# Routed experts in steps of two pairs of pages, in a hybrid block with two mixture-of-experts layers

## The chip, the cores and the metric

The kernel runs on one core of a Trainium2 chip. The metric is the device time of one execution in microseconds (us); three executions of the kernel before took 1439.03, 1439.33 and 1444.63 us, so its median is 1439.33 us. Five engines share the work: PE (TensorE, matrix products and transposes, with its weight loads shown as PEld), DVE (VectorE), ACT (ScalarE), POOL (GpSimd) and SP (SyncE, which here issues most DMA transfers). Each engine takes its instructions in order, and waits where an operand, a buffer or a bank of PSUM is not ready.

## The reference

`x` has shape 4 x 1024 x 256 in float32, so there are 4096 tokens of width 256. The block is

```python
x = x + attn_a(layernorm(x))     # RWKV time mixing
x = x + ffn(layernorm(x))        # mixture of experts, layer 1
x = x + attn_b(layernorm(x))     # retention, 16 heads
x = x + ffn(layernorm(x))        # the same experts, layer 2
```

and the part that is changed is the routed half of `ffn`, with E = 64 experts of inner width F = 64, of which each token takes K = 4:

```python
scores = softmax(flat @ router_w)
_, topk_idx = top_k(flat @ router_w + router_bias, 4)
comb = the four scores of each token, scaled to sum 1, at the chosen experts
g = silu(einsum('nd,edf->nef', flat, wg)); u = einsum('nd,edf->nef', flat, wu)
routed = einsum('ne,nef,efd->nd', comb, g * u, wd)
shared = two shared experts of width 256, for every token
```

## The kernel before

**Pages and pairs.** The 4096 tokens are handled in 8 segments of 512. A token's normalized row is sent, by four indirect writes from POOL (L429), to rows of a buffer in memory called `sent`, in pages of 128 rows where each page belongs to one expert. Two pages make a pair. Pair p is loaded, computed and stored as a unit by `routed` (L518), and the results land in a second buffer, `made`. Afterwards `gather` (L593) fetches four rows for each token back with indirect reads from POOL (L606), and DVE adds them into `x` with their weights (L617). How many pairs hold what segments 0 to i have sent is `until(i)`; the kernel uses the list `USUAL` (L75), 33, 38, 43, 51, 59, 67, 75, 83, when the drawn routing fits in it, which it does here in both layers (83 pairs each: 1328 instructions of L554 are 2 layers x 83 pairs x 8). A second arm of the program, not taken here, uses the worst case of 96 pairs.

**One pair.** `load` (L522) reads the two expert numbers of the pair, then has SP issue three DMA transfers: the rows `rx` (256 KB, L530) and the packed weights of its two experts `rw` (two of 192 KB, L532). `up` (L537) turns the rows with four PE transposes into one bank of PSUM (`rt`), which DVE copies to `rxT` (L546). `mid` (L549) multiplies by the gate and up weights (`rg`, half a bank: 2 pages x 128 columns), ACT takes silu of the gate half (`rs`, L559), DVE multiplies it by the up half (`rh`, L562), and ACT copies the product to the upper 64 partitions (L563), so that two products can use the two halves of the PE rows. `down` (L566) multiplies by the down weights into two half-filled banks (`rp`), which are copied to `ry` (L581): the first by ACT, the second by DVE for the first `until(0)` pairs and by ACT later. ACT then issues the store of 256 KB to `made` (L582).

**What sets the order.** `step(p)` (L584) records load(p), up(p-2), mid(p-3), down(p-4) at position p of a track, and `merge` (L54) interleaves tracks by their positions: in layer 1 with the gathers and with the retention batches, which start at position `until(0) + 14`; in layer 2 with the gathers, the stores of the output and the shared experts (`shared`, L446: L457, L462, L463, L470). From that recorded order a scheduler builds each engine's final order by its own model of durations, so neighbours can change places. A new tile of a tag waits until the tile that had its buffer is no longer read. `deep` gives the counts of buffers: in layer 1, (4, 2, 4) for `rx` and `rw`, for `ry`, and for the gathered rows; in layer 2, (6, 4, 6). `rxT`, `rs` and `rh` have two buffers each. Tag B has three banks of PSUM, used by `rt`, by both `rp` halves and by other stages; tag A has four.

`beat` (L79) notes a DVE instruction, and `on_beat` (L83) makes a POOL gather wait for the last one noted.

Of the kernel before, what the change touches and what calls it, by code (L numbers as in the profile page):

```python
# [10 lines left out]
F32 = mybir.dt.float32  # L11
# [10 lines left out]
P = 128  # L22
D = 256
KC = D // P
# [24 lines left out]
def track(steps, lo, hi):  # L49

    return [(lo + (hi - lo) * n / len(steps), step) for n, step in enumerate(steps)]
# [9 lines left out]
def hybrid_kernel(ctx: ExitStack, tc: tile.TileContext, a: dict, out: bass.AP):  # L61
# [94 lines left out]

    def pairs_until(i):

        return min(NPAIR, (((i + 1) * SEG * TOPK + E * (P - 1)) // P + 1) // 2)

    PACE, LAG = 2, 7.0

# [80 lines left out]
    class Ffn:  # L243
# [273 lines left out]

        def routed(self, pool, until):  # L518

            st, first, last = {}, until(0), until(NSEG - 1)  # L520

            def load(p):  # L522
# [7 lines left out]
                nc.sync.dma_start(out=x, in_=sent[p * P : (p + 1) * P])  # L530
                for j, e in enumerate(got):
                    nc.sync.dma_start(  # L532
# [1 line left out]
                    )  # L534
                st[p] = dict(x=x, w=w)

            def up(p):  # L537
                nm, s = f"{self.name}{p}", st[p]
                tp = bank("B", f"rt_{nm}", [P, KC, 2, P])
                for j in range(2):  # L540
                    for k in range(KC):
                        nc.tensor.transpose(  # L542
                            tp[:, k, j, :], s["x"][:, j, k * P : (k + 1) * P], ident
                        )
                xT = pool.tile([P, KC, 2, P], F32, tag="rxT", bufs=2, name=f"rxT_{nm}")
                beat(nc.vector.tensor_copy(out=xT, in_=tp))  # L546
                s["xT"] = xT

            def mid(p):  # L549
                nm, s = f"{self.name}{p}", st[p]  # L550
                gu = bank("A", f"rg_{nm}", [P, 2, P])
                for j in range(2):
                    for k in range(KC):
                        nc.tensor.matmul(  # L554
                            gu[:, j, :], lhsT=s["w"][:, j, k * 2 * F : (k + 1) * 2 * F],
                            rhs=s["xT"][:, k, j, :], start=(k == 0), stop=(k == KC - 1),
                        )
                act = pool.tile([P, 2, P], F32, tag="rs", bufs=2, name=f"rs_{nm}")
                nc.scalar.activation(out=act[F:], in_=gu[:F], func=AF.Silu)  # L559

                h = pool.tile([P, 2, P], F32, tag="rh", bufs=2, name=f"rh_{nm}")
                beat(nc.vector.tensor_mul(out=h[:F], in0=gu[F:], in1=act[F:]))  # L562
                nc.scalar.copy(out=h[F:], in_=h[:F])  # L563
                s["h"] = h

            def down(p):  # L566
                nm, s = f"{self.name}{p}", st.pop(p)
                y = pool.tile([P, 2, D], F32, tag="ry", bufs=self.deep[1], name=f"ry_{nm}")
                halves = [bank("B", f"rp_{nm}_{c}", [P, 2, P]) for c in range(2)]
                for j in range(2):  # L570

                    for c, yp in enumerate(halves):
                        r = slice(c * F, (c + 1) * F)
                        nc.tensor.matmul(  # L574
                            yp[:, j, :], lhsT=s["h"][r, j, :], rhs=s["w"][r, j, WD:],
                            start=True, stop=True,
                        )
                for c, yp in enumerate(halves):

                    copy = nc.vector.tensor_copy if c and p < first else nc.scalar.copy  # L580
                    copy(out=y[:, :, c * P : (c + 1) * P], in_=yp)  # L581
# [9 lines left out]
            return track([lambda p=p: step(p) for p in range(last + 4)], 0, last + 4)  # L591

        def gather(self, i, pool, until):  # L593


            nm, s = f"{self.name}{i}", self.pick[i]
            ready = [min(until(NSEG - 1), until(i) + PACE * t) for t in range(TT)]
            got = {}

            def fetch(t, k):  # L600
# [716 lines left out]
```

## Time and profile before

The profiled execution took 1439.49 us. Its span, from the first instruction to the last, is 1437.3 us; the rest, 2.2 us, lies around it.

| what | value |
|---|---|
| median of three executions | 1439.33 us (1439.03 to 1444.63) |
| profiled execution, and its span | 1439.49 us, 1437.3 us |
| stage with the time mixing and the first routing | about 0 to 385 us |
| layer 1, routed pairs nearly alone | about 390 to 520 us |
| layer 1, routed pairs among the retention batches | about 520 to 790 us |
| rest of the retention, routing for layer 2 | about 790 to 1120 us |
| layer 2, routed pairs and shared experts | about 1120 to 1411 us |
| last gathers, additions and stores | about 1411 to 1437 us |

The borders come from where the groups of L542, L554 and L574 are busy, asked in stretches of 20 us. A row of the groups' view has the line, the engine, the operation, the tile written and the tiles read, its size and count, then busy time, mean duration in ns, and the engine's idle time just before such instructions with what ended it. A matrix product in float32 runs as two PE instructions, so one `rg` product counts twice. PE durations in the groups overlap each other, since PE is pipelined; the chain of waits, which follows the last instruction back to what released each step, shows how long a run of them really holds the engine.

### The profile page before, as it was taken

The numbers are of one execution on the slowest core, as the hardware profiler recorded it, in microseconds if no ns is written. First come the engines' busy times: TensorE is split into PE (matmuls) and PEld (weight loads), VectorE is DVE, ScalarE is ACT, GpSimd is POOL, SyncE is SP. The second block draws the span as 40 slices with busy tenths as digits, with TensorE's granted clock in tenths as the row PEclk, the third lists the DMA queues.
The fourth block names the chain that finished last, engine by engine and source line by source line (L and its number), as shares of the span: only waits on it lengthen the run. The fifth ranks groups of instructions, "written<-read, shape, count | busy, mean of one in ns | idle before, by whom it ended". The sixth has DMA issues, their size and how long they took to land. (4 is left out here: it accounts for less than half of the span.)

```text
span 1437.3 us, 23813 instructions
## 1 busy us (share of the span) xinstructions
PE 1263.5 (88%) x7872; PEld 894.5 (62%) x7872; DVE 993.9 (69%) x2495; ACT 741.6 (52%) x1424; POOL 526.1 (37%) x536
## 2 busy tenths in 40 slices
PE   6899999999298879999999889699998799999993
PEld 2455555555277657777776666467465577777772
DVE  6999989998255447766666777886774355476664
ACT  7989898964044445556644463353431234444440
POOL 0043245545400144424224304536707000277565
PEclk9899999999699999999999999699999799999997
DMA  9976931112599976567453201212202798999984
GB/s 350 403 247 81 294 105 59 59 44 78 177 311 326 341 278 196 185 202 248 140 169 114 61 31 49 74 45 93 88 12 103 246 319 283 310 377 386 362 316 130
DMA packets 192297, 276.26 MB, mean 192 GB/s; under 512 B 53795, under 2 KB 119718, under 8 KB 192166
## 3 DMA queue, kind: packets, MB, share of 16 engines
q1 hardware_dynamic: 143686, 163.98, 36.0%
q0 software_dynamic: 24576, 67.14, 14.1%
q10 hardware_dynamic: 23904, 43.53, 8.0%
q8 instruction: 65, 1.06, 0.3%
q14 instruction: 66, 0.54, 0.1%
HBM read 166.05 MB, written 121.11 MB: 200 GB/s over the span
## 5 line engine op out<-in xcount | busy, mean ns | idle before, releaser
L606 POOL DMA_INDIRECT gy_f<-made,to_f x256 | 249.7, 975 | 486.8 <-DMA made<-ry_f 145.4
L429 POOL DMA_INDIRECT sent<-xn_f,to_f x256 | 273.4, 1068 | 413.9 <-issue 179.8
L554 PE MATMUL rg_f<-rxT_f,rw_f 128*128 128x128 f32 x1328 | 187.9, 285 | 11.6 <-DVE rxT_f L546 6.6
L554 PEld LDWEIGHTS rg_f<-rxT_f,rw_f 128*128 128x128 f32 x1328 | 167.1, 196 | 22.9 <-DVE rxT_f L546 14.8
L559 ACT ACTIVATE rs_f<-rg_f 64x256 f32<-64x256 f32 x166 | 62.2, 375 | 218.2 <-PE rg_f L554 193.7
L542 PE MATMUL rt_f<-ident,rx_f 128*128 128x128 f32 x664 | 108.0, 286 | 46.8 <-DMA rx_f<-sent 43.3
L574 PE MATMUL rp_f<-rw_f,rh_f 64*128 64x128 f32 x1328 | 140.1, 301 | 9.4 <-DVE S L1021 3.6
L546 DVE COPY rxT_f<-rt_f 128x512 f32<-128x512 f32 x166 | 114.3, 688 | 45.7 <-PE rt_f L542 44.2
L581 ACT COPY ry_f<-rp_f 128x256 f32<-128x256 f32 x266 | 92.9, 374 | 99.7 <-DMA made<-ry_f 50.5
L617 DVE SCALAR_TENSOR_TENSOR x<-gy_f,w_f,x 128x256 f32<-128x256 f32 x256 | 122.3, 482 | 14.3 <-DMA gy_f<-made,to_f 9.8
L457 PE MATMUL g_f<-xnT_f,f_swg 128*128 128x512 f32 x256 | 129.4, 623 | 0.6 <-ACT sh_f L462 0.6
L470 PE MATMUL o_f<-f_swd,sh_f 128*128 128x256 f32 x512 | 121.5, 385 | 8.2 <-DVE sh_f L463 4.3
L574 PEld LDWEIGHTS rp_f<-rw_f,rh_f 64*128 64x128 f32 x1328 | 103.4, 188 | 38.3 <-ACT ry_f L581 7.9
L457 PE MATMUL u_f<-xnT_f,f_swu 128*128 128x512 f32 x256 | 122.3, 595 | 0.7 <-DVE sh_f L463 0.7
L542 PEld LDWEIGHTS rt_f<-ident,rx_f 128*128 128x128 f32 x664 | 76.4, 144 | 71.5 <-issue 36.0
L562 DVE TENSOR_TENSOR rh_f<-rg_f,rs_f 64x256 f32<-64x256 f32 x166 | 70.7, 426 | 62.7 <-ACT rs_f L559 59.7
L470 PEld LDWEIGHTS o_f<-f_swd,sh_f 128*128 128x128 f32 x512 | 95.0, 191 | 29.9 <-DVE sh_f L463 6.7
L683 PE MATMUL rvk<-xnT_a,rvk 128*128 128x512 f32 x192 | 92.5, 629 | 7.1 <-DVE xnT_a L240 6.6
L1056 DVE TENSOR_TENSOR pm<-sc,decay 128x512 f32<-128x512 f32 x128 | 82.9, 681 | 17.9 <-PE sc L1035 17.7
L463 DVE TENSOR_TENSOR sh_f<-u_f,sh_f 128x512 f32<-128x512 f32 x64 | 43.8, 686 | 62.5 <-PE u_f L457 56.4
L462 ACT ACTIVATE sh_f<-g_f 128x512 f32<-128x512 f32 x64 | 38.0, 596 | 92.4 <-PE g_f L457 50.5
L563 ACT COPY rh_f<-rh_f 64x256 f32<-64x256 f32 x166 | 66.8, 403 | 33.9 <-DVE rh_f L562 29.7
(238 smaller groups left out, 2160.9 us busy)
## 6 DMA issues: line engine op xcount, KB each, us to landing
rw_f<-wx SPq DMA_DIRECT2D x332, 192.0 KB
rx_f<-sent SPq DMA_DIRECT2D x166, 256.0 KB
made<-ry_f ACTq DMA_DIRECT2D x166, 256.0 KB
sent<-zeros SPq DMA_DIRECT2D x7, 2048.0 KB
sent<-zeros SPq DMA_DIRECT2D x1, 10240.0 KB
x<-in_x_dram SPq DMA_DIRECT2D x8, 512.0 KB
wx<-in_wg_dram SPq DMA_DIRECT2D x2, 2048.0 KB
sent<-xn_f,to_f POOLq DMA_INDIRECT x256
```

Source lines behind the costliest of these rows:

```text
L429: ins = nc.gpsimd.indirect_dma_start(out=rows_sent[: pairs_until(i) * 2 * P, :], out_offset=bass.IndirectOffsetOnAxis(ap=st["to"][:, c : c ...
L457: nc.tensor.matmul(ps, lhsT=w[:, k, s], rhs=self.xnT[i][:, k, :], start=(k == 0), stop=(k == KC - 1),)
L470: nc.tensor.matmul(o[:, t, :], lhsT=st["h"][:, c, s], rhs=self.weights[2][:, c, :], start=(c == 0), stop=(c == NS - 1),)
L542: nc.tensor.transpose(tp[:, k, j, :], s["x"][:, j, k * P : (k + 1) * P], ident)
L546: beat(nc.vector.tensor_copy(out=xT, in_=tp))
L554: nc.tensor.matmul(gu[:, j, :], lhsT=s["w"][:, j, k * 2 * F : (k + 1) * 2 * F], rhs=s["xT"][:, k, j, :], start=(k == 0), stop=(k == KC - 1),)
L574: nc.tensor.matmul(yp[:, j, :], lhsT=s["h"][r, j, :], rhs=s["w"][r, j, WD:], start=True, stop=True,)
L581: copy(out=y[:, :, c * P : (c + 1) * P], in_=yp)
L606: ins = nc.gpsimd.indirect_dma_start(out=got[t][:, k, :], out_offset=None, in_=rows_made[: ready[t] * 2 * P, :], in_offset=bass.IndirectOf ...
L617: tc.keep_in_program_order(nc.vector.scalar_tensor_tensor(out=xs[i][:, t, :], in0=got[t][:, k, :], scalar=s["w"][:, c : c + 1], in1=xs[i][ ...
L683: nc.tensor.matmul(ps, lhsT=rvk[:, k, lo : lo + P], rhs=st["xnT"][:, k, :], start=(k == 0), stop=(k == KC - 1),)
L1056: ins = nc.vector.tensor_mul(out=pm, in0=ch[j]["sc"][g], in1=decay.rearrange("p (k g b) n -> p g k b n", k=KC, b=2)[:, g],)
```

## The change

Two pairs, q and q + 1, now go through `up`, `mid` and `down` together. Loads stay one pair at a time. The counts of pairs are rounded up to even numbers: `USUAL` becomes 34, 38, 44, 52, 60, 68, 76, 84; the worst case stays at 96. `rg`, and each half of `rp`, now fill a bank of 512 columns, and silu, the product, the copy of the product and the copies of `rp` are one instruction for two pairs. The `rt` banks and `rxT` stay one per pair. The store to `made` is one of 512 KB for two pairs. `rs` and `rh` have one buffer of twice the size. `ry` keeps two buffers in layer 1, each twice as large, and has two instead of four in layer 2. The buffers of `rx` and `rw` stay at four pairs in layer 1 and six in layer 2. `step` records, at odd positions p, up(p-3), then down(p-5), then mid(p-3), after load(p). The down products keep the order they are recorded in, after the first.

```diff
-    NPAIR = (NPAGE + 1) // 2
+    NPAIR = 2 * ((NPAGE + 3) // 4)
-    USUAL = [(max(E + 2 + 10 * i, (i + 1) * SEG * TOPK // P + E // 2 + 6) + 1) // 2 for i in range(NSEG)]
+    USUAL = [
+        2 * ((max(E + 2 + 10 * i, (i + 1) * SEG * TOPK // P + E // 2 + 6) + 3) // 4)
+        for i in range(NSEG)
+    ]
...
-                w = pool.tile([P, 2, WD + P], F32, tag="rw", bufs=self.deep[0], name=f"rw_{nm}")
+                w = pool.tile([P, 2, WD + P], F32, tag="rw", bufs=self.deep[3], name=f"rw_{nm}")
...
+            def up(q):
+                for p in (q, q + 1):
...
+            def mid(q):
+                nm = f"{self.name}{q}"
+                gu = bank("A", f"rg_{nm}", [P, 2, 2, P])
+                for i in range(2):
+                    s = st[q + i]
+                    for j in range(2):
+                        for k in range(KC):
+                            nc.tensor.matmul(
+                                gu[:, i, j, :], lhsT=s["w"][:, j, k * 2 * F : (k + 1) * 2 * F],
+                                rhs=s["xT"][:, k, j, :], start=(k == 0), stop=(k == KC - 1),
+                            )
+                act = pool.tile([P, 2, 2, P], F32, tag="rs", bufs=1, name=f"rs_{nm}")
                 nc.scalar.activation(out=act[F:], in_=gu[:F], func=AF.Silu)
-                h = pool.tile([P, 2, P], F32, tag="rh", bufs=2, name=f"rh_{nm}")
+                h = pool.tile([P, 2, 2, P], F32, tag="rh", bufs=1, name=f"rh_{nm}")
                 beat(nc.vector.tensor_mul(out=h[:F], in0=gu[F:], in1=act[F:]))
                 nc.scalar.copy(out=h[F:], in_=h[:F])
...
+                y = pool.tile([P, 2, 2, D], F32, tag="ry", bufs=self.deep[1], name=f"ry_{nm}")
+                halves = [bank("B", f"rp_{nm}_{c}", [P, 2, 2, P]) for c in range(2)]
+                for i in range(2):
+                    for j in range(2):
+                        for c, yp in enumerate(halves):
+                            r = slice(c * F, (c + 1) * F)
+                            ins = nc.tensor.matmul(
+                                yp[:, i, j, :], lhsT=h[r, i, j, :], rhs=two[i]["w"][r, j, WD:],
+                                start=True, stop=True,
+                            )
+                            if i or j or c:
+                                tc.keep_in_program_order(ins)
                 for c, yp in enumerate(halves):
-                    copy = nc.vector.tensor_copy if c and p < first else nc.scalar.copy
-                    copy(out=y[:, :, c * P : (c + 1) * P], in_=yp)
-                nc.scalar.dma_start(out=made[p * P : (p + 1) * P], in_=y)
+                    copy = nc.vector.tensor_copy if c and q < first else nc.scalar.copy
+                    copy(out=y[:, :, :, c * P : (c + 1) * P], in_=yp)
+                nc.scalar.dma_start(
+                    out=made[q * P : (q + 2) * P].rearrange("(i p) j d -> p i j d", p=P), in_=y
+                )
             def step(p):
                 if p < last:
                     load(p)
-                for d, f in ((2, up), (3, mid), (4, down)):
-                    if 0 <= p - d < last:
+                for d, f in ((3, up), (5, down), (3, mid)):
+                    if (p - d) % 2 == 0 and 0 <= p - d < last:
                         f(p - d)
...
-    f1 = Ffn("f1_", pf, keep, (4, 2, 4))
+    f1 = Ffn("f1_", pf, keep, (4, 2, 4, 4))
...
-        f2 = Ffn("f2_", pf, arm.enter_context(tc.tile_pool(name="keep2", bufs=NSEG)), (6, 4, 6))
+        f2 = Ffn("f2_", pf, arm.enter_context(tc.tile_pool(name="keep2", bufs=NSEG)), (6, 2, 6, 6))
```

More of the change, by code (lines that the diff above doesn't have):

```diff
@@ L157, in pairs_until @@
     def pairs_until(i):
-        return min(NPAIR, (((i + 1) * SEG * TOPK + E * (P - 1)) // P + 1) // 2)
+        return min(NPAIR, 2 * ((((i + 1) * SEG * TOPK + E * (P - 1)) // P + 3) // 4))
     PACE, LAG = 2, 7.0
@@ L535, in load @@
                 st[p] = dict(x=x, w=w)
[L537 to L558, printed above, removed]
+            def up(q):
+                for p in (q, q + 1):
+                    nm, s = f"{self.name}{p}", st[p]
+                    tp = bank("B", f"rt_{nm}", [P, KC, 2, P])
+                    for j in range(2):
+                        for k in range(KC):
+                            nc.tensor.transpose(
+                                tp[:, k, j, :], s["x"][:, j, k * P : (k + 1) * P], ident
+                            )
+                    xT = pool.tile([P, KC, 2, P], F32, tag="rxT", bufs=2, name=f"rxT_{nm}")
+                    beat(nc.vector.tensor_copy(out=xT, in_=tp))
+                    s["xT"] = xT
@@ new lines, in mid @@
+            def mid(q):
[4 more added lines that the diff above has]
+                    for j in range(2):
+                        for k in range(KC):
+                            nc.tensor.matmul(
[3 more added lines that the diff above has]
+                act = pool.tile([P, 2, 2, P], F32, tag="rs", bufs=1, name=f"rs_{nm}")
@@ L559, in mid @@
                 nc.scalar.activation(out=act[F:], in_=gu[:F], func=AF.Silu)
-                h = pool.tile([P, 2, P], F32, tag="rh", bufs=2, name=f"rh_{nm}")
+                h = pool.tile([P, 2, 2, P], F32, tag="rh", bufs=1, name=f"rh_{nm}")
                 beat(nc.vector.tensor_mul(out=h[:F], in0=gu[F:], in1=act[F:]))
                 nc.scalar.copy(out=h[F:], in_=h[:F])
[L564 to L577, printed above, removed]
-                for c, yp in enumerate(halves):
-                    copy = nc.vector.tensor_copy if c and p < first else nc.scalar.copy
-                    copy(out=y[:, :, c * P : (c + 1) * P], in_=yp)
-                nc.scalar.dma_start(out=made[p * P : (p + 1) * P], in_=y)
@@ new lines, in mid, with down @@
+                st[q]["h"] = h
+            def down(q):
+                nm, two, h = f"{self.name}{q}", [st.pop(q), st.pop(q + 1)], None
+                h = two[0]["h"]
+                y = pool.tile([P, 2, 2, D], F32, tag="ry", bufs=self.deep[1], name=f"ry_{nm}")
+                halves = [bank("B", f"rp_{nm}_{c}", [P, 2, 2, P]) for c in range(2)]
+                for i in range(2):
+                    for j in range(2):
+                        for c, yp in enumerate(halves):
[6 more added lines that the diff above has]
+                                tc.keep_in_program_order(ins)
+                for c, yp in enumerate(halves):
+                    copy = nc.vector.tensor_copy if c and q < first else nc.scalar.copy
+                    copy(out=y[:, :, :, c * P : (c + 1) * P], in_=yp)
+                nc.scalar.dma_start(
+                    out=made[q * P : (q + 2) * P].rearrange("(i p) j d -> p i j d", p=P), in_=y
+                )
@@ L586, in step @@
                     load(p)
-                for d, f in ((2, up), (3, mid), (4, down)):
-                    if 0 <= p - d < last:
+                for d, f in ((3, up), (5, down), (3, mid)):
+                    if (p - d) % 2 == 0 and 0 <= p - d < last:
                         f(p - d)
-            return track([lambda p=p: step(p) for p in range(last + 4)], 0, last + 4)
+            return [(p, lambda p=p: step(p)) for p in range(last + 5)]
         def gather(self, i, pool, until):
@@ L597, in gather @@
             ready = [min(until(NSEG - 1), until(i) + PACE * t) for t in range(TT)]
+            assert not any(r % 2 for r in ready)
             got = {}
```

## The prediction

> **What bounds the kernel now.** I read the page's shares of busy time first, then the busy time by stage, because an average over unlike stages says little, and then, inside the two routed stages, the waits and the chain of waits.
>
> ```profile
> span 1437.3 us, 23813 instructions
> ...
> PE 1263.5 (88%) x7872; PEld 894.5 (62%) x7872; DVE 993.9 (69%) x2495; ACT 741.6 (52%) x1424; POOL 526.1 (37%) x536
> ```
>
> ```profile
> core 0: us, PE busy (x) PEld busy (x) DVE busy (x) ACT busy (x) POOL busy (x), PEclk, DMA share, GB/s
> 390.00:505.00 115.00, 100.26 (x796) 83.00 (x796) 59.12 (x116) 46.11 (x123) 7.61 (x8) 0.96 0.96 326
> 505.00:800.00 295.00, 269.48 (x2169) 210.04 (x2170) 198.34 (x476) 157.19 (x338) 112.52 (x116) 0.96 0.58 187
> ...
> 1115.00:1245.00 130.00, 122.53 (x862) 95.82 (x863) 61.33 (x119) 47.37 (x120) 4.80 (x6) 0.95 0.87 285
> 1245.00:1411.00 166.00, 160.06 (x1096) 121.43 (x1095) 108.98 (x213) 75.69 (x198) 107.35 (x110) 0.99 0.97 348
> ```
>
> The reader is to see that ACT and DVE are busy a third to two thirds of both layer 2 rows, while PE is at 94 and 96 per cent. In layer 2 the chain of waits is PE work without holes:
>
> ```profile
> 1185.17 0.89 PE rg_f L554 x8
> 1186.06 0.65 PE rp_f L574 x8
> 1187.30 0.89 PE rg_f L554 x8
> 1188.19 0.65 PE rp_f L574 x8
> ```
>
> A pair starts 2.13 us after the one before: 0.89 `rg`, 0.65 `rp`, and 0.59 of `rt` between 1186.71 and 1187.30. **So layer 2 is bound by PE**: 83 pairs x 2.13 = 177 us, and five segments of shared experts fill the rest.
>
> The start of layer 1 (first row) is different: DMA is busy 96 per cent. From 400 to 480 us, 239 instructions of `rg` mean 29.9 pairs in 80 us, 2.68 us each, half a microsecond over PE's own 2.13. The waits of that stretch, then SP's and PE's timeline:
>
> ```profile
> ACT ry_f L581 <- DMA made<-ry_f: 39.8, 28, 2.9
> ```
>
> ```profile
> 429.80 0.88 SPq L532 DMA_DIRECT2D rw_f<-wx  x2
> 430.72 0.51 SPq L530 DMA_DIRECT2D rx_f<-sent  x1
> 432.17 0.86 SPq L532 DMA_DIRECT2D rw_f<-wx  x2
> ```
>
> ```profile
> 431.23 0.72 PE L574 MATMUL rp_f<-rw_f,rh_f 64*128 64x128 f32 x8
> 432.08 1.16 PE L554 MATMUL rg_f<-rxT_f,rw_f 128*128 128x128 f32 x8
> ...
> 435.86 0.63 PE L542 MATMUL rt_f<-ident,rx_f 128*128 128x128 f32 x4 [0.18 <-DMA rx_f<-sent]
> ```
>
> ACT waits for `ry`, that is for the store of two pairs earlier. SP issues the weights of pair p+4 as soon as the down product of pair p has released their buffer. The rows issued at 430.72 are those whose transposes wait until 435.86, so a transfer takes 5.1 us here, with two pairs' loads in the queues; at the start of layer 2, on quiet queues, the first `rx` took 2.7 us (issued 1117.87, used 1120.55).
>
> **The change part by part.** The PE work of a pair stays the same: the same products, of the same shape. Full banks save PE nothing.
>
> *Fewer instructions on ACT and DVE.* The rows:
>
> ```profile
> L559 ACT ACTIVATE rs_f<-rg_f 64x256 f32<-64x256 f32 x166 | 62.2, 375 | 218.2 <-PE rg_f L554 193.7
> L562 DVE TENSOR_TENSOR rh_f<-rg_f,rs_f 64x256 f32<-64x256 f32 x166 | 70.7, 426 | 62.7 <-ACT rs_f L559 59.7
> L462 ACT ACTIVATE sh_f<-g_f 128x512 f32<-128x512 f32 x64 | 38.0, 596 | 92.4 <-PE g_f L457 50.5
> L463 DVE TENSOR_TENSOR sh_f<-u_f,sh_f 128x512 f32<-128x512 f32 x64 | 43.8, 686 | 62.5 <-PE u_f L457 56.4
> ```
>
> Two products of 256 columns take 0.85 us, one of 512 takes 0.69 (L463): 0.16 saved per two pairs on DVE. Silu saves 2 x 0.375 - 0.60 = 0.15 on ACT, and the copies of `rh` and `rp` some 0.2 us each by the same step. The Trainium skill, Perfetto Trace Analysis, section Optimizing Scalar/DVE Operations, has two rules here. Grouping raises throughput if the engine is saturated; if it is not, but makes bubbles on another engine, smaller instructions may finish the work sooner. The busy rows decide for the second: 61 of 130 us on DVE and 47 on ACT. By the first rule 42 double steps x 0.65 us of ACT would make 27 us in a layer; by the rows this time is hidden under PE, and the gain is 0.
>
> *A longer chain from `rg` to `rp`.* Now silu starts 0.2 us after the last `rg`, then come 0.38 silu, 0.43 product, 0.40 copy. After the change it is 0.60, 0.69 and about 0.62 (an estimate: 0.40 plus the 0.22 by which silu grows), and DVE usually has a copy of `rxT` (0.69, L546) ahead. So the first `rp` can start about 2.3 us, the second, which needs the copy on the upper partitions, about 3.2 us after the last `rg`. What PE has in between is read from the order of the built program. Before, each pair has 2.1 us or more of other PE work there, against a chain of 1.6. After, 27 or so of layer 2's 42 double steps have 3 to 6 us, thanks to a shared expert's product. The other 13 to 15 have only 1.8 to 2.5 us, and in these `rg` also follows closely on its own transposes, where the timeline of layer 1 shows a hole of 0.33 us per pair until `rxT` is there. Bounds: 0 if the scheduler's filling works, 1.3 us (3.2 less 1.9) for each of 15 if nothing does, 20 us. I take 0.6 us for 14 steps, nearer the hole that the trace shows: **8 us in layer 2**. DVE's gathers come four in a row (4 x 0.48) and could add; they stand mostly where PE has shared work.
>
> *One more pair per layer.* 84 instead of 83. Layer 2 pays 2.13 us of PE. In layer 1 the retention starts at position 48 instead of 47, so 2.7 us at the rate of that stage.
>
> *Weights in layer 1: the same four buffers, released two pairs at a time.* Now PE has two whole pairs between the down product that frees a buffer and the `rg` that needs it refilled: 5.3 us at the present rate. After, the built order is, in turns, `rg` of step Q complete, down of Q-2, four plus four transposes, one down product of Q, the first half of the next `rg`, the rest of the down. Between the release and the `rg` that wants the new weights lie only about 2 us of PE work, less than the quiet 2.7 us transfer. So the loop closes through DMA: for two double steps, (0.1 wake, 0.45 to the second issue, 2.7) = 3.25 until half a step's weights are there, 0.89 `rg`, 0.56 of down; then, with four issues (1.35 us of SP), 4.15, 0.89, 0.65; and 0.3 of handoffs: 10.7 us for four pairs, which is what they take now (4 x 2.68). That is with quiet queues. With the loaded 5.1 us in both places it is 15.6. The queues hold less than now, since loads are released later, but four pairs still move 3.7 MB, 11.3 us at 325 GB/s. I take 11.1 us, near the lower end because the weights go first in each burst: 2.78 a pair, 0.1 x 47 = **4.7 us**, and with the added pair **7.4 us in layer 1**.
>
> *The store.* `ry` gets room for twice the rows in layer 1, so ACT's wait above goes; late next is the weights' loop, so it brings nothing there. In layer 2 the room is the same. At the end, POOL's last 16 gathers wait for the last store (1408.53, ended by it) and follow at about 1.25 us each up to the end; the last copies are two of 0.6 instead of two of 0.37, and 256 KB more are to land: 0.5 + 0.7, with 0.2 for the handoff **1.4 us**.
>
> *The mixed stage, 505 to 800 us.* Retention work of some 5 to 20 us stands between double steps and covers both chains. PE idles 25 us there; coarser lumps can make this better or worse: -5 to +8, taken as 0.
>
> **Sum:** 7.4 + 2.1 + 8 + 1.4 = 18.9 us, on 1439.5 of the profiled execution (the median shown, 1439.33, is the same): **1458 us**.
>
> **The rivals.** *(a) Holes filled:* weights no later than now, DVE and ACT chains covered by the reordered PE work. Then the added pairs and the end remain, 2.7 + 2.1 + 1.4: 1446. For it: 27 steps are covered already; against it, the 2 us of slack before `rg`. *(b) Faster:* the wait for `ry` is the true limit of layer 1's start. Before it sets in, down products start at 398.75, 401.13 and 403.51, 2.38 us apart. 48 x 2.38 less 47 x 2.68 is -11.7; with +3.5 for layer 2's pair and the end, and 2 us of relief on ACT in the mixed stage, 1429. It decides if a weights transfer takes under about 2.4 us, so that the loop falls below 9.5 us; against it stand the 2.7 us row and 96 per cent DMA. *(c) Loaded queues:* transfers of about 4 us in the loop, 13.3 us for four pairs, 3.33 each: +34 us in layer 1, 1485. For it: 5.1 us now; against: fewer loads in flight. *(d)* The change fills banks as it says, but as PE's work doesn't shrink, this is (a) again.
>
> **How the numbers follow.** My forecast has 0.62 (own range 1449 to 1470), (a) 0.19, (b) 0.07, (c) 0.12. Two runs of this kernel can be told apart from about 0.5 per cent, 7.2 us. Slower by more: the forecast, (c) and about half of (a), 0.82. Within: the other half, 0.11. Faster: (b), 0.07. The range from 1441 to 1481 leaves out (b), the low end of (a) and most of (c).
>
> **What would show it.** Right: between 400 and 480 us PE or PEld waits for `rw` in `rg`, ACT's wait for `ry` is gone, the DMA share is lower, and fewer than 29.9 pairs pass; in layer 2 PE idles before `rp` for `rh`, some 8 us in all; the last gather follows the last store as before. Wrong: 2.5 us a pair or less in that stretch, or no new holes in layer 2; or a retention stage more than 8 us off.

## The result and the profile after

The change makes the kernel slower: 1512.97 us (median of 4 executions, 1503.01 to 1518.05) against 1441.98 us (4 executions, 1439.03 to 1445.79), a ratio of 1.048 with a 95% interval of 1.041 to 1.055. The profiled execution took 1518.05 us. Some executions of every version run slower at a lower granted clock: ratios and their intervals leave these out, medians do not, so that a ratio need not be that of the two medians shown. The two lines of its page that answer to those shown of before:

```profile
span 1516.1 us, 23098 instructions
...
PE 1305.7 (86%) x7912; PEld 924.6 (61%) x7912; DVE 973.7 (64%) x2385; ACT 689.7 (45%) x1122; POOL 522.1 (34%) x536
```

ACT and DVE have less to do, as meant: 52 and 20 us. PE has 42 us more busy time, although it got only two more pairs. Where the time went is read from the first and last starts of three groups, the transposes `rt` of both layers and the first product of the retention (`sc`), in both traces. The column of e12 is a second profile of the changed kernel; e13 is an experiment below.

| stretch, us | before | changed | e12 | e13 |
|---|---|---|---|---|
| start to first `rt` | 391.4 | 397.2 | 395.2 | 393.3 |
| layer 1's start: first `rt` to first `sc` | 143.8 | 192.8 | 182.7 | 147.4 |
| retention and routing: first `sc` to first `rt` of layer 2 | 585.3 | 591.0 | 589.2 | 598.1 |
| layer 2: first to last `rt` | 274.7 | 292.5 | 290.7 | 277.5 |
| last `rt` to the end | 42.1 | 42.6 | 42.6 | 42.0 |
| span | 1437.3 | 1516.1 | 1500.4 | 1458.3 |

Of the 78.8 us, layer 1's start has 49.0 and layer 2 has 17.8; the 5.8 us ahead of the first `rt` and the 5.7 us of the third row were not traced to a cause. The busy time by stage, for these two stages (layer 2 in two parts, before and after its gathers set in):

```profile
core 0: us, PE busy (x) PEld busy (x) DVE busy (x) ACT busy (x) POOL busy (x), PEclk, DMA share, GB/s
400.00:540.00 140.00, 116.38 (x730) 95.37 (x728) 48.61 (x72) 31.68 (x54) 0.00 (x0) 0.80 0.70 231
...
1181.00:1312.00 131.00, 127.21 (x858) 97.51 (x858) 56.13 (x84) 35.83 (x60) 0.00 (x0) 0.97 0.84 275
1312.00:1473.00 161.00, 153.09 (x1037) 116.76 (x1036) 93.86 (x173) 58.40 (x102) 98.78 (x102) 0.98 0.99 347
```

In layer 1's start the DMA share fell from 0.96 to 0.70, and PE's granted clock (the share of its full clock that the trace shows as granted to it), which no step of the prediction speaks of, from 0.96 to 0.80. The waits from 405 to 541 us name the loop that the prediction described:

```profile
PE rg_f L561 <- DMA rw_f<-wx: 17.2, 20, 2.0
...
PEld rg_f L561 <- DMA rw_f<-wx: 6.5, 9, 2.2
```

`rg` waits for its weights, at most 2.0 us at a time, and ACT's wait for the store (39.8 us from 400 to 480 us before) is no longer among the waits. In layer 2 PE is still busy nearly throughout, yet its chain of waits reads differently. Before it was `rg` x8, `rp` x8, `rt` x4 in turn. Now:

```profile
1228.43 0.45 PE rg_f L561 x4
1228.87 0.41 PE rp_f L583 x2
1229.29 0.64 PE rg_f L561 x4
1229.93 1.09 PE rp_f L583 x14
1231.02 1.09 PE rg_f L561 x8
```

The down product of two pairs is in two pieces, one product (two instructions) and seven, with other work between. All but the first product are held in the order in which they are recorded; the first one is free, and the scheduler moves it ahead, to where the lower half of `rh` is ready and the copy to the upper half is not. In layer 2 this happens in 36 of 42 double steps. Two `rp` instructions hold PE for 0.41 us here, where eight held it for 0.65 before.

The rows of silu and of the product have the durations that were expected of them (0.60 and 0.69):

```profile
L566 ACT ACTIVATE rs_f<-rg_f 64x512 f32<-64x512 f32 x84 | 49.4, 588 | 179.3 <-PE rg_f L561 169.4 <-DMA rw_f<-wx 6.7 <-PE o_f L473 1.7
L569 DVE TENSOR_TENSOR rh_f<-rg_f,rs_f 64x512 f32<-64x512 f32 x84 | 58.2, 693 | 59.5 <-ACT rs_f L566 45.1 <-PE rp_f L583 12.7
```

### The profile page after: what moved, and what is told of

The parts are those of the page before. It is cut to its first block, busy times and chain, and to the rows that moved or that the text cites. A ratio compares the mean times of both kernels' runs of the same rounds, so it can differ in the third digit from the quotient of the medians.

```text
span 1516.1 us, 23098 instructions
## 1 busy us (share of the span) xinstructions
PE 1305.7 (86%) x7912; PEld 924.6 (61%) x7912; DVE 973.7 (64%) x2385; ACT 689.7 (45%) x1122; POOL 522.1 (34%) x536
## 5 line engine op out<-in xcount | busy, mean ns | idle before, releaser
L432 POOL DMA_INDIRECT sent<-xn_f,to_f x256 | 271.8, 1062 | 418.1 <-issue 182.7
L561 PE MATMUL rg_f<-rxT_f,rw_f 128*128 128x128 f32 x1344 | 208.9, 304 | 35.0 <-DMA rw_f<-wx 24.6
L561 PEld LDWEIGHTS rg_f<-rxT_f,rw_f 128*128 128x128 f32 x1344 | 177.5, 206 | 61.3 <-DVE rxT_f L551 21.2
L592 ACT COPY ry_f<-rp_f 128x512 f32<-128x512 f32 x134 | 73.6, 588 | 234.5 <-PE rp_f L583 219.4
L583 PE MATMUL rp_f<-rw_f,rh_f 64*128 64x128 f32 x1344 | 149.7, 316 | 21.5 <-DVE S L1035 10.8
L583 PEld LDWEIGHTS rp_f<-rw_f,rh_f 64*128 64x128 f32 x1344 | 117.4, 209 | 57.4 <-issue 27.4
L566 ACT ACTIVATE rs_f<-rg_f 64x512 f32<-64x512 f32 x84 | 49.4, 588 | 179.3 <-PE rg_f L561 169.4
L569 DVE TENSOR_TENSOR rh_f<-rg_f,rs_f 64x512 f32<-64x512 f32 x84 | 58.2, 693 | 59.5 <-ACT rs_f L566 45.1
L570 ACT COPY rh_f<-rh_f 64x512 f32<-64x512 f32 x84 | 51.8, 617 | 79.5 <-DVE rh_f L569 77.0
L592 DVE COPY ry_f<-rp_f 128x512 f32<-128x512 f32 x34 | 23.5, 691 | 95.8 <-PE rp_f L583 95.8
L460 PEld LDWEIGHTS u_f<-xnT_f,f_swu 128*128 128x128 f32 x256 | 48.4, 192 | 57.2 <-issue 52.2
```

What stands on the lines that cost most here:

```text
L432: ins = nc.gpsimd.indirect_dma_start(out=rows_sent[: pairs_until(i) * 2 * P, :], out_offset=bass.IndirectOffsetOnAxis(ap=st["to"][:, c : c ...
L460: nc.tensor.matmul(ps, lhsT=w[:, k, s], rhs=self.xnT[i][:, k, :], start=(k == 0), stop=(k == KC - 1),)
L561: nc.tensor.matmul(gu[:, i, j, :], lhsT=s["w"][:, j, k * 2 * F : (k + 1) * 2 * F], rhs=s["xT"][:, k, j, :], start=(k == 0), stop=(k == KC ...
L583: ins = nc.tensor.matmul(yp[:, i, j, :], lhsT=h[r, i, j, :], rhs=two[i]["w"][r, j, WD:], start=True, stop=True,)
L592: copy(out=y[:, :, :, c * P : (c + 1) * P], in_=yp)
```

## The experiments

**How they are compared.** Chips differ. On those that ran e1 to e11, e15 and e16 the kernel before itself takes 1580 to 1618 us; the chip of e12 to e14 is like the first (1438.84 us). So whole times are given as ratios to the kernel before on the same chip. Causes are read from two stretches in which the chips nearly agree: the *start of layer 1*, from 8 us after the first `rt` to the first gather, and the *quiet part of layer 2*, from 10 us after its first `rt` to its first gather there. In each, the time from the start of one PE instruction to the start of the next was summed over `rt`, `rg` and `rp`, and divided by the pairs that passed. The kernel before has 2.73 and 2.11 us by this count; with single pairs on the other chips it is 2.65 to 2.86 and 2.10 to 2.11. Pairs are counted by `rg`, which is coarse for double steps: one more of them at the edge of the quiet part changes its figure by some 5 per cent. So the last column divides each tile's time by that tile's own count, and there the chips agree within 0.01 us.

| kernel | layer 1's start, us per pair | granted clock there | layer 2 quiet, us per pair | the same, each tile by its own count |
|---|---|---|---|---|
| before | 2.73 | 1.00 | 2.11 | 2.11 |
| changed: first, e12, e15, e5 | 3.84, 3.55, 3.70, 3.49 | 0.81, 0.93, 0.89, 0.97 | 2.34, 2.33, 2.24, 2.24 | 2.30, 2.30, 2.30, 2.31 |
| e1, double steps in layer 1 only | 3.64 | 0.93 | 2.11 | 2.11 |
| e2, double steps in layer 2 only | 2.86 | 0.98 | 2.25 | 2.30 |
| e3, six `rw` buffers | 2.91 | 0.98 | 2.26 | 2.30 |
| e4, even counts only | 2.76 | 1.00 | 2.10 | 2.11 |
| e6, down first | 3.01 | 0.97 | 2.23 | 2.30 |
| e7, e6 with filler | 3.04 | 0.97 | 2.23 | 2.30 |
| e8, upper half first | 3.45 | 0.99 | 2.08 | 2.14 |
| e10, e2 with the upper half first | 2.69 | 1.00 | 2.11 | 2.14 |
| e11, before with four `ry` buffers | 2.65 | 1.00 | 2.10 | 2.11 |
| e13, both mended | 2.88 | 1.00 | 2.12 | 2.12 |
| e14, layer 2 only, whole down products | 2.73 | 1.00 | 2.14 | 2.12 |
| e16, changed with filler in the wait | 3.31 | 0.99 | 2.26 | 2.30 |

The start of layer 1 is counted by `rg`, in e16 by `rp`, because its filler writes to `rg`'s bank.

### e1 and e2: one layer at a time

Both have both versions of `routed` (`routed_one` is that of before) and the even counts. In e1 `second_layer` calls the version of before (with 4 buffers of `ry`), in e2 `first_layer` does.

```diff
# e1
-            f2.routed(pr, until), *gathers, stores, track(side, 0.5, n - 4),
+            f2.routed_one(pr, until), *gathers, stores, track(side, 0.5, n - 4),
# e2
-                f1.routed(pr, until), *f1.gathers(pg, until), [s for s in batches if s[0] < cut]
+                f1.routed_one(pr, until), *f1.gathers(pg, until), [s for s in batches if s[0] < cut]
```

> Double steps in layer 1 only; layer 2 keeps single pairs (with 4 buffers for ry), counts even in both. If the loss sits where the trace of the changed kernel shows it, in the start of layer 1 (first retention product some 55 to 60 us late), this costs 50 to 60 us: 1492 to 1502, and layer 2 is again a chain of PE work without holes. Rival, that the two layers lose alike through the longer chain from rg to rp: 1470 to 1478. My prediction's own split would give 7.4 in layer 1 and 2.1 for the pair in layer 2: 1451.

> Single pairs in layer 1, double steps in layer 2 only, counts even in both. By the trace of the changed kernel layer 2 lost some 18 us, and an added pair in layer 1 costs 2.7: 1458 to 1464, with the granted clock of layer 1's start back at 1.00. My prediction's terms (2.7 + 2.1 + 8 + 1.4) give 1456. Rival, alike in both layers: 1470 to 1478.

Measured: e1 1659.88 us, 1.031 (1.018 to 1.044) times before; e2 1630.72 us, 1.015 (1.005 to 1.025). As ratios to 1442 us the expectations were 1.035 to 1.042 and 1.011 to 1.015, and the rival's 1.019 to 1.025 in both. The intervals are too wide to shut the rival out, and e4 below has 1.012 with no double step at all. The table decides: each layer's stretch changes only where its own steps are doubled, 3.64 and 2.11 in e1, 2.86 and 2.25 in e2, so the loss is mostly layer 1's, and loss alike in both layers is out. One thing goes against a loss in layer 2 on these chips: from its first to its last `rt` pass 329.6 us in e1 and 329.0 in e4, with single pairs, but 321.8 in e2, with double steps, because PE idles 42 us there in e4 and 31 in e2. So a pair costs more in the quiet part on every chip, but layer 2 as a whole is seen to get longer only on the first chip and the one like it; why PE idles more with single pairs on the others was not traced.

### e3: more buffers for the weights

```diff
-    f1 = Ffn("f1_", pf, keep, (4, 2, 4, 4))
+    f1 = Ffn("f1_", pf, keep, (4, 2, 2, 6))
```

> The changed kernel with 6 instead of 4 buffers of rw in layer 1 (and, to make room, 2 instead of 4 buffers for gathered rows there, which the start of layer 1 does not use). Weights theory: the refill comes in time, between 410 and 500 us a pair takes 2.9 us or less instead of 3.8, the clock there is 0.95 or more, the waits of rg for rw shrink below 3 us, and the first retention product comes 35 to 55 us earlier than in the changed kernel; the whole is 1460 to 1480 unless the gathers suffer. Chain theory (one rs and one rh buffer, four steps in a row from rg to rp): a pair still takes 3.5 us or more there, the clock stays under 0.85, and the time stays within 10 us of 1513.

Measured: 1636.0 us, 1.020 (1.007 to 1.032). Layer 1's start takes 2.91 us per pair, and from its first `rt` to the first `sc` pass 152.2 us, against 186.4 in e1, which has the changed kernel's layer 1 on the same chip, and 158.6 in e4. That is 34 us earlier; 35 to 55 had been expected. Silu, the product, the copy and their single buffers are the same as in the changed kernel. So the loss there is the weights' loop and not the chain from `rg` to `rp`.

### e4: even counts alone

The kernel before with the changed `NPAIR`, `USUAL` and `pairs_until` and nothing else.

> The kernel before with the counts made even and nothing else: one more pair in each layer and a retention that starts one position later. Prediction's terms: 2.7 + 2.1 = 4.8 us, 1445 to 1449. Rival, that the shifted positions reorder the mixed stage: more than 10 us either way.

Measured: 1631.78 us, 1.012 with an interval of 0.999 to 1.025. It cannot tell 5 us from none. That both stretches keep their rate (2.76 and 2.10) says that a pair costs what it did before, so two added pairs should cost about 2.7 and 2.1; that sum was not measured by itself.

### e5 to e8: the loop's order, a filler, and the split

e5 is the changed kernel unchanged. e6 holds `rg` behind the whole down product of two pairs earlier, in layer 1's start:

```diff
+                            ins = nc.tensor.matmul(
                                 gu[:, i, j, :], lhsT=s["w"][:, j, k * 2 * F : (k + 1) * 2 * F],
                                 rhs=s["xT"][:, k, j, :], start=(k == 0), stop=(k == KC - 1),
                             )
+                            if self.name == "f1_" and 4 <= q < first + 14:
+                                tc.keep_in_program_order(ins)
```

e7 adds to e6, ahead of each `rp` there, six products of `ident` with itself into the bank that `rp` then overwrites. e8 takes the upper half of `rh` first, so that the one product which is free to move has to wait for the same copy as the others:

```diff
-                        for c, yp in enumerate(halves):
+                        for c, yp in reversed(list(enumerate(halves))):
...
-                            if i or j or c:
+                            if i or j or not c:
```

> The changed kernel as it is, to stand beside the next three on one chip, because a chip can run every version of this program some 12 per cent slower, as the first four experiments showed. Expected 1.04 to 1.055 times the kernel before if the chip is like the first, with 3.6 to 3.9 us for a pair in the start of layer 1.

> The changed kernel with rg of layer 1's start held behind the whole down product of two pairs earlier, so that between the release of a weight buffer and the rg that wants it refilled lie rg, two rt and rp of other pairs (some 4 us of PE work) instead of some 2, and rp is not split. Weights theory: the waits of rg for rw fall to less than half, a pair takes 3.3 us or less instead of 3.76; PE now waits for rh before rp instead, 1 to 2 us for two pairs. Chain theory: that wait takes the place of the other in full, and a pair takes 3.6 us or more.

> As the run before, with 6 unused products of ident (some 1.3 us of PE at full clock) ahead of each rp in layer 1's start, where PE waits for rh. Clock theory: the low granted clock there comes from PE's holes and costs time in the loop; with the holes filled the clock rises to 0.95 or more, and a pair takes no longer, or up to 0.5 us less, although work was added. Rival, that the clock is only a sign: a pair takes 0.2 to 0.6 us more, and the whole is 5 to 25 us slower.

> The changed kernel with the down product that needs the upper half of rh first. The first product is the only one that the scheduler may move; it then waits for the same copy as the others, and the built order of layer 2 splits rp into 1 + 7 products 13 times instead of 36. Split theory: in layer 2 of the changed kernel each split costs some 0.4 us (PE leaves the 64-row products twice, 0.2 us each), so layer 2 gets 7 to 10 us shorter. Chain theory: the splits fill holes that the longer chain makes, so layer 2 stays within 3 us or gets longer, with waits of rp for rh. Layer 1's start changes by less than 15 us.

Measured, with 1606.68 us for the kernel before: e5 1650.52 us, 1.027 (1.018 to 1.037), less than on the first chip and than expected, as are its 3.49 us for a pair; e6 1637.02 us; e7 1639.13 us, 1.023 (1.014 to 1.031); e8 1643.57 us, 1.021 (1.013 to 1.028). On this chip the retention and the gathers take longer whatever the kernel, which hides part of the change; the stretches tell more.

In e6 a pair takes 3.01 instead of 3.49 us, and `rg` no longer waits for `rw`. Another wait has come, as either theory said; from 430 to 530 us:

```profile
PE rp_f L585 <- DVE rh_f L571: 18.6, 16, 1.2
```

It is 1.2 us per double step. The wait that it replaces was longer, so the weights theory holds here too, and the chain costs something as soon as it is bare. e7 adds some 1.3 us of PE work per double step, and a pair takes 3.04 us, so that this work lay almost wholly in the wait. Of the clock e7 tells nothing: it had 1.00 from 440 to 500 us in e6 already.

In e8 layer 1's start stays (3.45), while layer 2's quiet part goes from 2.24 to 2.08 us per pair (2.31 to 2.14 by own counts), with 13 splits instead of 36, and the stretch from its first to its last `rt` from 321.2 to 314.5 us. These 6.7 us are just under what the split theory said (7 to 10), and against the chain theory (within 3).

### e9: the change of kind by itself

To the kernel before, after all its work, products of a tile of `x` with itself are appended: *full* ones (128 rows, like `rg`) and *half* ones (64 rows, lower and upper by turns, like `rp`), in a fixed order, with nothing to wait for in between.

```diff
+    for _ in range(6):
+        fulls(8)
+        halves(8)
...
+        fulls(6)
+        halves(1)
+        fulls(2)
+        halves(7, 1)
...
+    for _ in range(12):
+        fulls(4)
+        halves(4)
```

> The kernel before with a run of products appended that nothing reads: full products (128 rows, as rg) and half products (64 rows, as rp), in blocks of 8 full + 8 half six times, then 6 + 1 half + 2 + 7 half six times, then 4 + 4 twelve times. Split theory: products of one kind take 0.11 and 0.08 us each, and each time PE leaves a block of half products costs 0.15 to 0.25 us more: 8 + 8 takes 1.6 to 1.7 us per turn at full clock, 6 + 1 + 2 + 7 takes 0.2 to 0.45 us more. Rival, that the change of kind is free and the pieces in the chain are hidden waits for rh and rxT: both patterns take the same within 0.05 us.

The chain of waits, first for 8 + 8, then for 6 + 1 + 2 + 7, then for 4 + 4 (a product is two instructions):

```profile
1577.64 1.09 PE half L1268 x16
1578.73 1.98 PE full L1260 x16
...
1596.99 1.53 PE full L1260 x12
1598.53 0.42 PE half L1268 x2
1598.94 0.64 PE full L1260 x4
1599.58 1.08 PE half L1268 x14
...
1627.02 0.65 PE half L1268 x8
1627.67 1.09 PE full L1260 x8
```

The clock is 1.00 in all of them. A turn of 8 + 8 takes 1.09 + 1.98 = 3.07 us. The same products with one half product moved take 1.53 + 0.42 + 0.64 + 1.08 = 3.67 us: **0.60 us for one split**. Two turns of 4 + 4 take 3.48. (The expectation's totals counted an instruction where a product has two; its difference of 0.2 to 0.45 was too small.) Long runs of one kind show where this comes from: 48 full instructions took 5.55 us, 0.116 each, and 80 half ones 4.67 us, 0.058 each. By these rates a block of 16 full ones has 0.13 us over, one of 4 0.18, a block of 16 half ones 0.16, one of 2 0.30. So every block here, of 2 to 16 instructions, costs 0.13 to 0.3 us besides its work. This program was run once. Nothing waits here, so the pieces in layer 2's chain need no hidden wait to explain them.

### e10 and e11: two parts alone

e10 is e2 with the edit of e8. e11 is the kernel before with `f1 = Ffn("f1_", pf, keep, (4, 4, 4))`, four buffers of `ry` in layer 1.

> Single pairs in layer 1 and double steps in layer 2 only, there with the down product of the upper half first, so that rp stays whole in most steps. Split theory: layer 2 takes 6 to 10 us less from its first to its last transpose than in the run with layer 2 only, and the whole stands at 1.00 to 1.012 times the kernel before. Chain theory: no gain against that run (1.015).

> The kernel before with 4 instead of 2 buffers of ry in layer 1, so that ACT's wait for the store goes and nothing else. My rival (b) said that this wait is the true limit of layer 1's start: then a pair takes 2.4 us there instead of 2.68 and the whole is 10 to 14 us faster. If the loads are the limit (DMA busy 96 per cent), the wait moves to rx or rw and the whole changes by less than 4 us.

Measured, with 1587.49 us for the kernel before: e10 1601.97 us, 1.017 (1.008 to 1.026), no gain on e2's 1.015 by the whole, although the quiet part of layer 2 went from 2.25 to 2.11 us per pair (2.30 to 2.14), and layer 2 from its first to its last `rt` from 321.8 to 315.0 us, the 6 to 10 that the split theory said. The intervals are wider than the 7 us in question, so the whole settles nothing here. e11 took 1585.54 us (20 executions), 0.995 (0.992 to 0.999): faster by half a per cent, and a pair takes 2.65 us. ACT's wait for the store did cost something, but the rate goes to 2.65 and not to 2.4, so rival (b)'s limit is out. The start of layer 1 explains only some 2 us of the gain (e10, with two buffers and single pairs there on the same chip, has 2.69); where the rest arises was not traced. e11 is the one version that is faster than both kernels.

### e12 to e14: both causes mended

e12 is the changed kernel once more. e13 has e3's buffers and e8's order, and its second `rp` bank from tag C, so that the second product need not wait for a bank that `rt` still holds; all 42 down products of layer 2 are then whole in the built order. e14 has the same down product in layer 2, and single pairs with four buffers of `ry` in layer 1.

```diff
-                halves = [bank("B", f"rp_{nm}_{c}", [P, 2, 2, P]) for c in range(2)]
+                halves = [bank("BC"[c], f"rp_{nm}_{c}", [P, 2, 2, P]) for c in range(2)]
```

> The changed kernel once more, for the share of the low clock in layer 1's start: the first profile had 0.69 to 0.91 there and 3.84 us for a pair, the second 0.97 and 3.49. If the clock adds to the loop, the time of a pair follows the clock of its profile (3.4 to 3.6 us at 0.95 or more, 3.7 or more under 0.85); if the clock is only a sign, 3.4 to 3.6 whatever the clock.

> The changed kernel with 6 buffers of rw in layer 1 (and 2 for gathered rows there), the upper half first in the down product, and the second bank of rp from tag C, so that in the built order of layer 2 all 42 down products are whole. If the weights loop and the splits are the two causes: layer 1's start takes 2.95 us or less for a pair, layer 2's quiet stretch 1.95 to 2.10 us for a pair instead of 2.24 to 2.34, and the whole is 1.00 to 1.015 times the kernel before. If the chain from rg to rp is a cause of its own, the quiet stretch stays at 2.2 or more, with waits of rp for rh.

> Layer 1 as before with single pairs (even counts, 4 buffers of ry), layer 2 in double steps with whole down products as in the run ahead. By the measured switch costs a double step of whole blocks takes 0.87 + 1.98 + 1.09 = 3.94 us against 2 x 2.11 before: 0.28 us for each of 42 double steps, 12 us, of which the two added pairs take back 4.8, and ry gives 5 to 8: 0.988 to 0.998 times the kernel before. If holes of the chain take the gain, 1.00 to 1.015.

Measured, with 1438.84 us for the kernel before: e12 1509.40 us, 1.050 (1.046 to 1.054); e13 1464.59 us, 1.020 (1.015 to 1.024); e14 1447.56 us, 1.005 (1.002 to 1.008). e12's clock of 0.93 lies between the two cases of its expectation, so it decides nothing about the clock. e13 takes back 45 of 71 us; its layer 1 came as expected, its quiet part (2.12 against 1.95 to 2.10) and its whole (1.020 against 1.00 to 1.015) just missed. Its stages of layer 1's start and of layer 2:

```profile
401.00:503.00 102.00, 78.72 (x720) 67.66 (x720) 48.89 (x73) 32.10 (x55) 0.01 (x1) 1.00 0.95 314
1149.00:1263.00 114.00, 110.92 (x840) 88.17 (x839) 53.97 (x81) 35.54 (x61) 0.23 (x1) 1.00 0.90 294
```

DMA is at 0.95 again and the clock at 1.00. The first table shows both stages within 3.6 and 2.8 us of the kernel before, which is about one added pair each. What remains is mostly in the retention stage (598.1 us, 9 more than in e12), where two instead of four buffers for gathered rows are the likely cause: POOL's gathers wait 153.2 us there for DVE's additions, which free these buffers, and 35.2 in e12. That was not tried alone. In the chain of layer 2 the down product is whole:

```profile
1201.88 0.87 PE rt_f L547 x8
1202.75 1.09 PE rp_f L583 x16
1203.84 1.98 PE rg_f L561 x16
```

These three make 3.94 us for two pairs, 0.32 less than 2 x 2.13. Yet e13 and e14 take 2.12 us per pair (by own counts) and not 1.97: `rt`, which by this line needs 0.44 per pair, has 0.57 until the next instruction starts, since PE now waits for `rh` or `rxT` in some steps. So the longer chain is real, some 0.14 us per pair; it takes the gain of the fuller blocks, and e14 came out at 1.005, in the branch that was expected if holes take the gain.

### e15 and e16: the clock

e16 puts three products that read only `rxT` and `ident` ahead of each half of `rg` in layer 1's start, into the part of the bank that `rg` then overwrites; e15 is the changed kernel on the same chip.

```diff
                     s = st[q + i]
+                    for n in range(3):
+                        if self.name == "f1_" and 4 <= q < first + 14:
+                            nc.tensor.matmul(
+                                gu[:, i, 0, :], lhsT=s["xT"][:, 0, 0, :], rhs=ident, start=True, stop=True,
+                            )
```

> The changed kernel beside the next run, on the same chip: about 1.05 times the kernel before where that takes 1439 us, with a granted clock of 0.78 to 0.95 in layer 1's start and 3.5 to 3.8 us for a pair.

> The changed kernel with 3 unused products (0.66 us at full clock) ahead of each half of rg in layer 1's start, where PE waits for rw; the order around them is nearly that of the changed kernel. They need no weights, so they run inside the wait. If the low clock comes from these holes and lengthens the loop, the clock there rises to 0.97 or more and a pair takes 3.3 to 3.5 us, 5 to 20 us less for the whole than the run ahead if that has a clock under 0.93. If the clock is only a sign, a pair takes as long as in the run ahead or up to 0.4 us more. If the clock of the run ahead is 0.95 or more, this pair of runs tells nothing of it.

Measured, with 1579.96 us for the kernel before: e15 1633.48 us, 1.036 (1.029 to 1.044); e16 1613.64 us, 1.025 (1.019 to 1.030). More work, and the kernel is faster. The stage in e15, then in e16:

```profile
425.00:545.00 120.00, 94.77 (x654) 76.51 (x654) 45.00 (x67) 29.12 (x49) 0.00 (x0) 0.88 0.73 244
```

```profile
425.00:545.00 120.00, 112.19 (x930) 98.54 (x926) 46.94 (x70) 33.09 (x56) 6.84 (x8) 0.99 0.84 279
```

The clock rose from 0.88 to 0.99; over the whole of all four executions each it was 0.901 to 0.911 in e15 and 0.916 to 0.924 in e16. The same windows asked for `rp` alone have 256 instructions in 120 us in e15, 3.75 us per pair, and in e16, from 445 to 525 us at a clock of 1.00, 194 in 80 us, 3.30 us per pair. PE's waits for `rw` in these 80 us of e16 are down to 3.2 us. e15's own trace shows the clock's part with no edit between: from `rp` to `rp`, two double steps (four pairs) take 15.9, 16.7 and 15.9 us from 443 to 492 us, at a clock of 0.70 to 0.76, and 14.0, 13.3, 14.7 and 13.4 us from 492 to 547 us, at 1.00. So the low clock is no mere sign: it lengthens the products in the loop. At a full clock the loop takes 3.30 us per pair with filler and some 3.46 without, so not all of e16's gain is the clock's. It stays open what makes the clock fall: e15's stayed at 1.00 from 483 us on, in the same loop, although PE's waits then came to 13.0 us (492 to 547) against 7.2 (443 to 492).

## Why the prediction was wrong in size

The sign was right and the mechanism of layer 1 was named, but the sum was 18.9 us where the medians differ by 71.0 and the spans of the profiles by 78.8.

**"Weights in layer 1", 4.7 of 7.4 us, measured 49.0 (38.9 in e12).** This is the step that failed, in two terms. The first is the loop, of which the prediction said "I take 11.1 us" for four pairs; e16 measures 4 x 3.30 = 13.2, and e15 at a full clock 13.3 to 14.7. SyncE's and PE's timeline of e12 show the mis-sized parts:

```profile
438.60 2.68 SPq L536 DMA_DIRECT2D rw_f<-wx  x4
...
443.30 3.66 SPq L536 DMA_DIRECT2D rw_f<-wx  x4
...
452.70 2.67 SPq L536 DMA_DIRECT2D rw_f<-wx  x4
```

```profile
442.33 1.16 PE L583 MATMUL rp_f<-rw_f,rh_f 64*128 64x128 f32 x14
444.71 0.68 PE L561 MATMUL rg_f<-rxT_f,rw_f 128*128 128x128 f32 x4 [1.22 <-DMA rw_f<-wx]
445.82 0.71 PE L561 MATMUL rg_f<-rxT_f,rw_f 128*128 128x128 f32 x4 [0.43 <-DMA rw_f<-wx]
```

Four issues in a row take 2.68 to 3.66 us, 0.67 to 0.92 each instead of 0.45, and a transfer's median in the changed kernel's stretch is 3.2 us instead of 2.7. The issues are not all that SP does there: between the second and the third it reads the second pair's expert numbers (L528, 0.49 us in the median), which the sum left out, and single issues take from 0.34 up to 0.86 us. With these the prediction's own sum becomes (0.1 + 0.67 + 3.2 + 0.89 + 0.56) + (0.1 + 3 x 0.67 to 0.92 + 3.2 + 0.89 + 0.65) + 0.3 = 12.6 to 13.3 us. Choosing the value "near the lower end because the weights go first in each burst" was the error, and 11.1 is even less than the 11.3 us that the prediction itself gives for moving four pairs; rival (c), at 13.3, had the loop right. (Its figure for loaded queues, 15.6, should read 15.5: 10.7 and twice 2.4.) Against the 2.68 of before this is (3.30 - 2.68) x 47 + 3.30 = 32 us, or 40 with e15's 3.46. The second term was in no rival: the granted clock. At 0.81 a pair took 3.84 us, so of the 49.0 us an estimated 9 to 17 are the clock's (49.0 less 40 or 32), and in e12, at 0.93, at most 7.

**"The PE work of a pair stays the same ... Full banks save PE nothing": wrong both ways.** The products are the same, but each block of a kind costs 0.13 to 0.3 us besides. By e9, whole blocks of two pairs would save PE 0.41 us per double step (3.48 less 3.07), and split ones cost 0.19 more than before (3.67 less 3.48).

**"A longer chain from rg to rp", 8 us of holes in layer 2, where 17.8 us were lost with the added pair: the form was wrong.** PE's time in layer 2 from the first to the last `rt`, each instruction counted up to the start of the next, and waits over 0.15 us apart:

| us | before | changed | e13 |
|---|---|---|---|
| `rp` | 55.0 | 61.0 | 45.1 |
| `rg` | 80.8 | 84.9 | 84.1 |
| `rt` | 40.4 | 41.9 | 43.3 |
| `o` | 28.9 | 33.6 | 27.7 |
| `g`, `u` | 62.7 | 59.5 | 60.2 |
| idle | 6.8 | 11.6 | 17.1 |

Idle time, the step's own term, grew by only 4.8 us, and 4.1 of that lie in one place, where `rp` waits behind DVE's additions:

```profile
1373.57 0.49 PE L583 MATMUL rp_f<-rw_f,rh_f 64*128 64x128 f32 x2 [1.76 <-DVE rh_f L569]
1376.41 2.05 PE L583 MATMUL rp_f<-rw_f,rh_f 64*128 64x128 f32 x14 [2.36 <-DVE rxT_f L551]
```

The scheduler did fill the other holes, with `rg`, `o` and the first down product, and the filling is what costs: `rp`, `rg` and `rt` take 11.6 us more, some 1.5 of it for the part of the added pair that lies in this stretch, and `o`, much of which now stands between pieces, 4.7 us. e9's price alone, 36 splits x 0.19 = 7 us, is too low for this; the rest of it was not measured apart. The prediction's lower bound, "0 if the scheduler's filling works", had no price on the filling. In e13, where every down product is whole, idle time grows by 10.3 us. That is near the 8 that were forecast, but in part by luck: 7.4 us of it are waits of `rg` for `rxT`, and before `rp` stand 7.6 (2.7 before). And `rp` takes 9.9 us less, the saving that the prediction put at nothing.

**The other steps.** The added pair per layer fits what remains in e13 (3.6 and 2.8 us, predicted 2.7 and 2.1), though in layer 2 that is also the balance of the table above. ACT's and DVE's shorter work brought nothing by itself, as said. ACT's wait for `ry` went, and the weights were late next. The end was set at 1.4 us and measured 0.5. The mixed stage was bounded at -5 to +8 and came with the retention to +5.7. Of the signs named beforehand, the waits for `rw`, the lower DMA share and the fewer pairs came; of the 8 us of holes before `rp` 3.4 came (6.1 us of idle time there against 2.7). Rival (b) was wrong as a forecast; by e11, doing away with the wait it named is worth half a per cent.

**Open.** What makes the clock fall; the part of the filling's cost that e9's price leaves over; and why layer 2 as a whole is shorter with double steps on the slower chips. e10's whole shows no gain where its layer 2 does, and the cause of e13's longer retention stage was not tried alone.

## What to carry to other kernels

When buffers are released in larger lumps, count the engine's work between a release and the need of the refilled buffer, take transfer and issue times from bursts of the new size, not from single transfers, and count what else the issuing engine does between two issues; a loop that closes through DMA is paid in full, and a low clock of PE in it is paid on top. Bigger instructions free an engine that was not the limit, and lengthen the chain to the one that was. A hole that a scheduler fills with other work is not free where the work changes its kind: look at how many blocks of a kind PE gets, not only at how many products.

## What the runs showed of the hardware that was not expected

- A change between products of 128 and of 64 rows costs PE 0.13 to 0.3 us per block, with no wait in sight (e9, one execution); half products of alternating halves run at 0.058 us per instruction, full ones at 0.116.
- PE's granted clock in layer 1's start fell to 0.81 although no wait of PE there was longer than 2.03 us. The trace's clock is either 0.5 or 1.0 and changes on multiples of 3.41 us. The Trainium skill, TensorE: Matmul & The Clock Gate, section HAM oscillation, gives as its abstract rule that PE should have no gaps of more than about 3.4 us; here the clock fell with shorter ones. Idle time alone does not decide either: e13 had PE idle for 23 of 102 us in that stretch at a clock of 1.00, the changed kernel for 24 of 136 at 0.81, and its other three profiles, with the same loop, had 0.93, 0.89 and 0.97.
- Filling such holes with unused products made the kernel 1.2 per cent faster (1613.64 against 1633.48 us).
- The kernel before took 1439 us in the first runs and on the chip of e12 to e14, and 1580 to 1618 on four others. Single instructions were as long: in e11 `rg` has a median of 275 ns and silu of 376, before 275 and 375. The longer stages were those with gathers and retention: in e11 656.5 and 324.3 us for the third and fourth row of the first table, before 585.3 and 274.7.
